# Attention with packed heads: maxima rounded and sums divided on GpSimd, the first causal mask added by the array

## The chip, the cores and the metric

One NeuronCore of a Trainium2 chip runs the whole program in one launch. The metric is the device time in microseconds. Engines are named as the profile names them: PE (TensorE; PEld is its loading of weights), DVE (VectorE), ACT (ScalarE), POOL (GpSimd) and SP (SyncE, which only issues DMAs here).

## The reference

A network of four layers on 2048 tokens of width 128, in float32. Each layer is half a feed-forward block, an attention and half a feed-forward block, each behind a layer norm and added to x. Only the first three attentions are touched:

```python
# attn0: 8 heads of 16, causal, geometry term in the keys; attn1, attn2: 16 heads of 8
scores = q @ k.T * scale            # attn2 with rotary tables
scores = scores + causal            # attn0 only
out = softmax(scores) @ v
x = x + out @ w_out                 # attn1 also + bias
```

The sequence is all 2048 tokens as one in each of them. attn3 (16 heads of 64, causal, with a latent key and value) runs in the same function but isn't changed.

## The kernel before, in words

`packed` prepares attn0, attn1 and attn2 and `flash` runs them. Tokens are taken in 4 chunks of 512. Heads are handled in groups of 4, so an iteration is one group of 4 heads and one chunk of queries: 8 iterations in attn0 (2 groups, heads of 16), 16 in each of attn1 and attn2 (4 groups, heads of 8). Scores are made twice.

The first pass (`stream_a`, `some`) finds the maximum of every row. PE multiplies 128 queries by 512 keys for two heads at once into a pair of PSUM banks, of which there are two pairs (L1071). VectorE reduces a pair to one maximum per row and head (L1089). In attn0's diagonal chunk the last 128 columns must be masked: there VectorE runs, for each head, one operation that adds a strip of zeros and of the mask and takes the maximum (L1081). At the end of an iteration `maxima` reduces the four partial maxima (L1100) and `put_max` writes the negated maximum as a bf16 value and a bf16 remainder into `top` (L1556, L1557). Some program time later `put` lets PE form the shifted queries in a bank named pm, as the queries plus the transposed maxima (L1566, L1570), and ScalarE copies them to q2 (L1574).

The second pass (`stream_b`) makes the scores again with keys on the partitions and the maximum already subtracted (L1213), ScalarE takes the exponential (L1222), and PE multiplies by the values into one accumulator bank (L1159). The products with the values of a key tile are issued in two halves, one key tile later. A column of ones among the values gives the sum of each row. Banks for L1213, for pm and for the transposes are taken in turn out of the same three.

At the end of an iteration `finish` copies the accumulator (L1582, ScalarE). `normal` transposes it into a bank po (L1587), takes the reciprocal of the sums (L1592, VectorE) and multiplies (L1593, VectorE) into `os`, the output with all heads of a chunk. After the last group `out_a` transposes that on PE (L1607) and `out_b` projects it and adds it to x (L1615, L1620).

PE's instructions stay in program order. `flash` writes that order by hand: it keeps a clock of the columns issued so far, takes a step of the first pass whenever that pass is less than an iteration and a bit ahead of the second, and calls pending work (`after(delay, fn)`) once the clock has passed its time. The other engines' order comes from the scheduler, which also follows the few order-only dependencies (`in_order`); every engine then works through its own queue in order. `half_masks` (L1026) is attn3's way to mask: two heads with 64 rows each get the bf16 mask added in their banks by products with an identity, in halves of the rows.

Most lines of the changed file stand 2 to 10 lines away from those of the one before; line numbers here are those of the kernel before.

Of the kernel before, what the change touches and what calls it, by code (L numbers as in the profile page):

```python
# [9 lines left out]
F32 = mybir.dt.float32  # L10
# [54 lines left out]
def tile_macaron(ctx: ExitStack, tc: tile.TileContext, a: dict, out: bass.AP, stages=STAGES):  # L65
# [31 lines left out]
    nc.gpsimd.memset(ones, 1.0)  # L97
    minus_half = const.tile([P, TC], F32, name="minus_half")
    nc.gpsimd.memset(minus_half, -0.5)

    def cs(name):
        return cst[:, slice(*CONSTS[name])]
# [871 lines left out]
    def flash(io, pool, early, its, nh, causal, scale, s1, s2, pv_mm, put_max, begin, finish, poll=None,  # L974
# [7 lines left out]

        halved = nh == 2
        clock = [0.0]
        total = [0]
        later = []

# [7 lines left out]
        def after(delay, fn):  # L995
            later.append((clock[0] + delay, fn))
            later.sort(key=lambda v: v[0])
# [7 lines left out]
        def chunks(qc):  # L1005
            return qc + 1 if causal else NC

        if halved:

            halves = {}  # L1010
            for name in ("ident", "maskq", "maskk"):
                raw = pool().tile([P, 2, P], F32, name="halfraw", tag="halfraw", bufs=2)
                for j in range(2):
                    nc.sync.dma_start(
                        out=raw[P // 2 * j : P // 2 * (j + 1)],
                        in_=a["consts"][:, slice(*CONSTS[name])].rearrange("(b i) k -> i b k", b=2),
                    )
                halves[name] = pool().tile([P, 2, P], BF16, name="half" + name)
                nc.vector.tensor_copy(halves[name], raw)

        def half_masks(outs, mask):

            for b in range(2):
                for j in range(2):
# [1 line left out]
                    pe(nc.tensor.matmul(  # L1026
                        outs[j], halves["ident"][s, b], halves[mask][s, b], start=False, stop=b == 1
                    ))

        if tiled and causal:  # L1030
            junk = pool().tile([P, CH], F32, name="junk")
            strip = pool().tile([P, CH], F32, name="strip")
            nc.gpsimd.memset(strip[:, : CH - P], 0.0)
            nc.vector.tensor_copy(strip[:, CH - P :], cs("maskq"))

        ready = set()
        alive = [True]
# [16 lines left out]
        def some(n, turns, mp):  # L1054

            g, qc = its[n]
            nk = chunks(qc)
            for first, (r, kcs) in enumerate(turns):
                before = hook(n, kcs[0], r) if hook is not None else None
                if first == 0 and before is None:  # L1060
                    before = newest[0]
                for kc in kcs:
                    for j0 in range(0, nh, 2):
                        ps = first_pass_bank()
                        last = causal and kc == qc
                        masked = last and not tiled
                        w = (r + 1) * P if last else CH
                        for j in range(2):
                            o = j * CH
                            lhsT, rhs = s1(n, j0 + j, r, kc)  # L1070
                            pe(nc.tensor.matmul(  # L1071
                                ps[:, o : o + w], lhsT, rhs[:, :w], start=True, stop=not masked
                            ))
                            pos[0] += w
                        if masked:
                            half_masks([ps[:, j * CH + w - P : j * CH + w] for j in range(2)], "maskq")
                        both = ps.rearrange("p (j n) -> p j n", j=2)
                        with tc.high_priority() if not waiting[0] else nullcontext():
                            if last and tiled:
                                for j in range(2):  # L1080
                                    ins = nc.vector.tensor_tensor_reduce(  # L1081
                                        junk[:, :w], both[:, j, :w], strip[:, CH - w :], 1.0, NEG,
                                        ALU.add, ALU.max, mp[:, r, j0 + j, kc : kc + 1],
                                    )
                                    if before is not None:
                                        in_order(ins, before)
                                        before = None
                            else:
                                ins = nc.vector.tensor_reduce(  # L1089
                                    mp[:, r, j0 : j0 + 2, kc], both[:, :, :w], AX.X, ALU.max,  # L1090
                                )
                        if before is not None:
                            in_order(ins, before)
                            before = None
                        yield 2 * w if tiled else w

        def maxima(n, mp):
            nk = chunks(its[n][1])
            mx = pool().tile([P, TC, nh], F32, name="mx", tag="mxa", bufs=3)
            nc.vector.tensor_reduce(mx, mp[:, :, :, :nk], AX.X, ALU.max, negate=True)  # L1100
            put, newest[0] = put_max(n, mx, pe)

            def done():
                put()
                ready.add(n)

            after(2000.0, done)

        newest = [None]
        waiting = [False]  # L1110
# [214 lines left out]
    def packed(io, early, hd, causal, scale, project, w, wv, wo, bias=None, outs=True):  # L1325
# [222 lines left out]
            o = (kt * 4 + j) * slot  # L1548
            return vt[its[n][0]][:, o : o + 32], slice(32 * j, 32 * j + 32)

        def put_max(n, mx, pe):
            top = tops[n % 3]
            tv = top.rearrange("p a r (j s) -> p a r j s", s=span)[:, :, :, :, 3:8:4]
            for i in range(nq):
                m = mx[:, :, i * per : (i + 1) * per]
                nc.vector.tensor_copy(tv[:, i, :, :, 0], m)  # L1556
                last = nc.vector.tensor_tensor(  # L1557
                    tv[:, i, :, :, 1], m, tv[:, i, :, :, 0], ALU.subtract
                )

            def put():

                t = room[0].tile([P, nq, CH], F32R, name="q2", tag="q2", bufs=3)
                for i in range(nq):
                    ps = bank("pm")
                    pe(nc.tensor.matmul(  # L1566
                        ps, masks_b["ident_r"], qt[its[n]][:, i, :], start=True, stop=False
                    ))
                    for r in range(TC):
                        pe(nc.tensor.matmul(  # L1570
                            ps[:, r * P : (r + 1) * P], top[:, i, r, :], masks_b["ident_b"],
                            start=False, stop=r == TC - 1,
                        ))
                    nc.scalar.copy(t[:, i, :], ps)  # L1574
                q2[its[n]] = t

            return put, last

        def finish(n, pv, after, pe):
            g, qc = its[n]  # L1580
            ov = room[1].tile([P, CH], F32, name="ov", tag="ov", bufs=2)
            nc.scalar.copy(ov, pv)  # L1582

            def normal():
                ps = bank("po")
                for r in range(TC):
                    pe(nc.tensor.transpose(  # L1587
                        ps[:, r * P : (r + 1) * P], ov[:, r * P : (r + 1) * P], ident
                    ))
                po = ps.rearrange("p (r j m) -> p r j m", r=TC, j=4)  # L1590
                rc = room[0].tile([P, TC, 4], F32, name="rc", tag="rc", bufs=2)
                nc.vector.reciprocal(rc, po[:, :, :, hd])  # L1592
                nc.vector.tensor_tensor(  # L1593
                    os[qc][:, :, g * 4 * hd : (g + 1) * 4 * hd].rearrange(
                        "p r (j d) -> p r j d", j=4
                    ),
                    po[:, :, :, :hd],
                    rc.unsqueeze(3).to_broadcast([P, TC, 4, hd]),
                    ALU.mult,
                )  # L1600
                if g == n_groups - 1:
                    after(OUT_A if causal else 1500.0, out_a)

            def out_a():
                ps = bank("oT")
                for i in range(TC):
                    pe(nc.tensor.transpose(ps[:, i * P : (i + 1) * P], os[qc][:, i, :], ident))  # L1607
                oT = room[1].tile([P, CH], F32, name="oT", tag="ov", bufs=2)
                nc.scalar.copy(oT, ps)
                after(1500.0, lambda: out_b(oT))  # L1610

            def out_b(oT):
                ps = bank("py").rearrange("p (i c) -> p i c", i=TC)
                for i in range(TC):
                    pe(nc.tensor.matmul(  # L1615
                        ps[:, i, :], oT[:, i * P : (i + 1) * P], wo, start=True, stop=True
                    ))
                if bias is not None:
                    nc.gpsimd.tensor_tensor(xs[qc], xs[qc], over(bias, TC), ALU.add)
                nc.vector.tensor_tensor(xs[qc], xs[qc], ps, ALU.add)  # L1620
                io.mark(qc)

            after(1500.0, normal)
# [766 lines left out]
```

## Time and profile before

| | |
|---|---|
| time of three runs, median (lowest to highest) | 3719.4 us (3716.38 to 3719.66) |
| the profiled execution's own time | 3720.81 us |
| its span, first to last instruction | 3719.1 us |
| mean granted PE clock | 0.950 |
| attn0, about 178 to 455 us | 277 us |
| attn1, about 793 to 1484 us | 691 us |
| attn2, about 1679 to 2391 us | 712 us |
| a maximum over two heads of 512 (L1089) | 1344 of them, 1219 ns each |
| masked maxima of attn0 (L1081) | 128 of them, 0.29 to 0.69 us each |
| exponential of 512 (L1222) | 2272 of them, 609 ns each |
| rounding of maxima in attn1 and attn2 (L1556, L1557) | 32 of each, about 0.20 and 0.23 us |
| reciprocal and product in attn1 and attn2 (L1592, L1593) | 32 of each, 0.26 and 0.29 us |

In the profile's groups the columns are line, engine, operation, output and inputs with their shapes, the count, the busy time in us with the mean of one in ns, and the idle time of the engine just ahead of such instructions, with what ended it. In a timeline they are start, length, engine, line, operation; a bracket gives idle time and what ended it. Neighbours of one line are merged ("x7"), and two instructions of one engine may overlap by some tens of ns, so that the spacing of starts, not the length of one, tells the pace.

### The profile page before, as it was taken

How to read it: one execution, taken by the hardware profiler on the slowest of the kernel's cores; microseconds unless marked ns; L12 is line 12 of the kernel's file. 1: busy time of each engine (PE TensorE's matmuls, PEld its weight loads, DVE VectorE, ACT ScalarE, POOL GpSimd, SP SyncE). 2: the span in 40 equal slices, each digit the busy share in tenths (PEclk: the TensorE clock that was granted, in tenths of full speed). 3: DMA queues.
4: the chain of work that ended last, by engine and by line, in shares of the span. 5: the costliest groups of instructions: out<-in, count | busy, mean ns of one | idle time of the engine just before them, and what ended most of it. 6: DMA issues, size and time to landing. Idle time of an engine off the chain costs nothing. (4 is left out here: it accounts for less than half of the span.)

```text
span 3719.1 us, 64518 instructions
## 1 busy us (share of the span) xinstructions
PE 3404.5 (92%) x25325; PEld 1837.3 (49%) x25325; DVE 2853.9 (77%) x4729; ACT 2025.6 (54%) x3815; POOL 817.1 (22%) x816
## 2 busy tenths in 40 slices
PE   7689987989999999997999999898889999999989
PEld 5543366854333333883333333376444444445457
DVE  6588556778999995778999999544777877788852
ACT  3346722317888888333888888731333344444442
POOL 1511124000000000210000000232555445533341
PEclk9779989979999999996999999898999999999999
DMA  3420123000000000100000000012443232211010
GB/s 106 98 52 14 37 62 91 7 20 9 15 6 16 6 4 7 55 25 21 10 16 10 12 6 1 26 44 68 151 146 112 96 106 98 97 57 52 24 35 12
DMA packets 124977, 170.18 MB, mean 46 GB/s; under 512 B 25152, under 2 KB 52930, under 8 KB 124672
## 3 DMA queue, kind: packets, MB, share of 16 engines
q1 hardware_dynamic: 122112, 160.80, 13.8%
q0 software_dynamic: 2560, 5.25, 0.9%
q8 instruction: 199, 3.26, 0.4%
q14 instruction: 106, 0.87, 0.1%
HBM read 101.25 MB, written 45.87 MB: 40 GB/s over the span
## 5 line engine op out<-in xcount | busy, mean ns | idle before, releaser
L1089 DVE TENSOR_REDUCE mp<-s 128x2 f32<-128x1024 f32 (+3 forms) x1440 | 1627.7, 1183 | 80.2 <-PE s L1071 56.7
L1222 ACT ACTIVATE pt<-s 128x512 f32<-128x512 f32 (+1 forms) x2368 | 1220.5, 601 | 217.7 <-PE s L1213 165.2
L1213 PE MATMUL s<-q,km 32*128 32x512 f32 (+2 forms) x2368 | 735.0, 493 | 28.8 <-ACT pt L1222 18.6
L1159 PE MATMUL pv<-pt,v 128*32 128x256 f32 (+1 forms) x8568 | 732.2, 414 | 22.9 <-ACT ov L1582 11.2
L1071 PE MATMUL s<-km,qt 32*128 32x512 f32 (+3 forms) x2368 | 617.1, 506 | 64.9 <-DVE mp L1089 45.3
L1213 PEld LDWEIGHTS s<-q,km 32*128 32x128 f32 (+1 forms) x2368 | 323.9, 184 | 531.4 <-issue 339.5
L1202 ACT ACTIVATE pt<-s 128x512 f32<-128x512 f32 (+3 forms) x640 | 306.3, 530 | 361.3 <-PE s L1194 216.3
L143 POOL TENSOR_TENSOR rs<-rs,minus_half 128x4 f32<-128x4 f32 x56 | 57.3, 1023 | 1491.8 <-DVE rs L142 1468.1
L2071 DVE TENSOR_TENSOR sum<-sum,pt 128x512 f32<-128x512 f32 (+3 forms) x328 | 260.0, 808 | 86.9 <-ACT pt L1202 85.6
L1159 PEld LDWEIGHTS pv<-pt,v 128*32 128x32 f32 x8568 | 169.2, 108 | 317.7 <-issue 147.1
L1194 PE MATMUL s<-q,k 64*128 64x512 f32 (+3 forms) x1920 | 295.1, 400 | 14.9 <-ACT pt L1202 10.5
L1159 PE MATMUL pv<-pt,latv 128*64 128x512 f32 (+3 forms) x1280 | 307.5, 560 | 1.3 <-ACT pt L1202 1.3
L2071 POOL TENSOR_TENSOR sum<-sum,pt 128x512 f32<-128x512 f32 (+1 forms) x200 | 264.7, 1324 | 179.8 <-ACT pt L1202 176.4
L1071 PEld LDWEIGHTS s<-km,qt 32*128 32x128 f32 (+1 forms) x2368 | 236.2, 191 | 123.8 <-DVE mp L1089 82.3
L1194 PEld LDWEIGHTS s<-q,k 64*128 64x128 f32 x1920 | 159.1, 186 | 222.8 <-issue 140.5
L715 ACT ACTIVATE sg<-pg 128x1024 f32<-128x1024 f32 x72 | 74.0, 1027 | 158.2 <-PE pg L229 142.0
L1071 PE MATMUL s<-k,q 64*128 64x512 f32 (+3 forms) x640 | 131.9, 430 | 19.0 <-DVE mp L1089 18.8
L1873 DVE TENSOR_TENSOR rot<-rot,tab 128x512 f32<-128x512 f32 x128 | 87.8, 686 | 74.8 <-PE rot L229 43.3
L725 PEld LDWEIGHTS pd<-l1d,h 128*128 128x128 f32 x1152 | 139.0, 191 | 5.6
L725 PE MATMUL pd<-l1d,h 128*128 128x128 f32 x1152 | 139.8, 275 | 0.0
L717 DVE TENSOR_TENSOR h<-pu,sg 128x1024 f32<-128x1024 f32 x72 | 87.8, 1220 | 51.7 <-PE pu L229 46.5
L1888 ACT CAST h<-rot 128x512 fp32r<-128x512 f32 x64 | 39.6, 619 | 159.5 <-POOL rot L1883 159.5
(572 smaller groups left out, 4736.3 us busy)
## 6 DMA issues: line engine op xcount, KB each, us to landing
tab<-in_l3rope SPq DMA_DIRECT2D x66, 256.0 KB
q<-q SPq DMA_DIRECT2D x32, 512.0 KB
k<-k SPq DMA_DIRECT2D x32, 512.0 KB
l0e<-in_l0e SPq DMA_DIRECT2D x32, 256.0 KB
q<-h SPq DMA_DIRECT2D x32, 256.0 KB
q<-rot SPq DMA_DIRECT2D x32, 256.0 KB
k<-h SPq DMA_DIRECT2D x32, 256.0 KB
k<-rot SPq DMA_DIRECT2D x32, 256.0 KB
```

Source lines behind the costliest of these rows:

```text
L715: nc.scalar.activation(sg, pg, AF.Silu)
L717: nc.vector.tensor_tensor(h.rearrange("p m n -> p (m n)"), pu, sg, ALU.mult)
L725: nc.tensor.matmul(pd[:, i, :], h[:, m, i * P : (i + 1) * P], wd[:, m, :], start=m == 0, stop=m == 1,)
L1071: pe(nc.tensor.matmul(ps[:, o : o + w], lhsT, rhs[:, :w], start=True, stop=not masked))
L1089: ins = nc.vector.tensor_reduce(mp[:, r, j0 : j0 + 2, kc], both[:, :, :w], AX.X, ALU.max,)
L1159: i = pe(nc.tensor.matmul(pv[out_rows, lo:hi], lhsT, pts[j][:, lo:hi], start=kt == 0, stop=kt == nt - 1 and hi == CH))
L1194: pe(nc.tensor.matmul(outs[j][:, c0:], lhsT, rhs[:, c0:], start=i == 0, stop=i == len(terms[0]) - 1 and not diag,))
L1202: ex = nc.scalar.activation(pts[j][:, c0:], outs[j][:, c0:], AF.Exp, scale=scale)
L1213: pe(nc.tensor.matmul(ps[:, c0:], lhsT, rhs[:, c0:], start=i == 0, stop=i == len(terms) - 1 and (tiled or not diag),))
L1222: ex = nc.scalar.activation(pt[:, c0:], ps[:, c0:], AF.Exp, scale=scale)
L1873: nc.vector.tensor_tensor(t.bitcast(F32), ps, halves["tabs"][i], ALU.mult)
L2071: eng.tensor_tensor(t[:, c0:], other[:, c0:], pts[j][:, c0:], ALU.add)
```

## The change

In attn0 the diagonal banks of the first pass are masked by `half_masks`, as in attn3, and reduced like all others, two heads at once. The junk and strip tiles go; two masks in bf16 are loaded and cast when attn0 begins.

In attn1 and attn2, from the second iteration on, `put_max` runs on GpSimd, and the put of the shifted queries is due 3000 instead of 2000 ns of program time after the maxima. In all iterations but the last, `normal` lets ScalarE copy the transposed accumulator out of PSUM, and GpSimd raises the sums to the power of -1 and multiplies.

```diff
+    minus_one = const.tile([P, TC, 4], F32, name="minus_one")
+    nc.gpsimd.memset(minus_one, -1.0)
...
+        aside = tiled and not causal
...
-        if halved:
+        if causal:
             halves = {}
-            for name in ("ident", "maskq", "maskk"):
+            for name in ("ident", "maskq", "maskk")[: 3 if halved else 2]:
...
-        if tiled and causal:
-            junk = pool().tile([P, CH], F32, name="junk")
-            strip = pool().tile([P, CH], F32, name="strip")
-            nc.gpsimd.memset(strip[:, : CH - P], 0.0)
-            nc.vector.tensor_copy(strip[:, CH - P :], cs("maskq"))
...
-                        masked = last and not tiled
+                        masked = last
...
-                            if last and tiled:
-                                for j in range(2):
-                                    ins = nc.vector.tensor_tensor_reduce(
-                                        junk[:, :w], both[:, j, :w], strip[:, CH - w :], 1.0, NEG,
-                                        ALU.add, ALU.max, mp[:, r, j0 + j, kc : kc + 1],
-                                    )
...
-                            else:
-                                ins = nc.vector.tensor_reduce(
-                                    mp[:, r, j0 : j0 + 2, kc], both[:, :, :w], AX.X, ALU.max,
-                                )
+                            ins = nc.vector.tensor_reduce(
+                                mp[:, r, j0 : j0 + 2, kc], both[:, :, :w], AX.X, ALU.max,
+                            )
...
-            nc.vector.tensor_reduce(mx, mp[:, :, :, :nk], AX.X, ALU.max, negate=True)
-            put, newest[0] = put_max(n, mx, pe)
+            newest[0] = nc.vector.tensor_reduce(mx, mp[:, :, :, :nk], AX.X, ALU.max, negate=True)
+            if aside and n:
+                put, _ = put_max(n, mx, pe, nc.gpsimd)
+            else:
+                put, newest[0] = put_max(n, mx, pe)
...
-            after(2000.0, done)
+            after(3000.0 if aside and n else 2000.0, done)
...
-        def put_max(n, mx, pe):
+        def put_max(n, mx, pe, eng=nc.vector):
...
-                nc.vector.tensor_copy(tv[:, i, :, :, 0], m)
-                last = nc.vector.tensor_tensor(
-                    tv[:, i, :, :, 1], m, tv[:, i, :, :, 0], ALU.subtract
-                )
+                eng.tensor_copy(tv[:, i, :, :, 0], m)
+                last = eng.tensor_tensor(tv[:, i, :, :, 1], m, tv[:, i, :, :, 0], ALU.subtract)
...
+                if causal or n == len(its) - 1:
...
+                else:
+                    ot = room[1].tile([P, CH], F32, name="ot", tag="ov", bufs=2)
+                    nc.scalar.copy(ot, ps)
+                    po = ot.rearrange("p (r j m) -> p r j m", r=TC, j=4)
+                    rc = room[0].tile([P, TC, 4], F32, name="rc", tag="rc", bufs=2)
+                    nc.gpsimd.tensor_tensor(rc, po[:, :, :, hd], minus_one, ALU.pow)
+                    nc.gpsimd.tensor_tensor(
+                        out, po[:, :, :, :hd],
+                        rc.unsqueeze(3).to_broadcast([P, TC, 4, hd]), ALU.mult,
+                    )
```

More of the change, by code (lines that the diff above doesn't have):

```diff
@@ L1078, in some @@
                         with tc.high_priority() if not waiting[0] else nullcontext():
-                            if last and tiled:
-                                for j in range(2):
-                                    ins = nc.vector.tensor_tensor_reduce(
-                                        junk[:, :w], both[:, j, :w], strip[:, CH - w :], 1.0, NEG,
-                                        ALU.add, ALU.max, mp[:, r, j0 + j, kc : kc + 1],
-                                    )
-                                    if before is not None:
-                                        in_order(ins, before)
-                                        before = None
-                            else:
-                                ins = nc.vector.tensor_reduce(
-                                    mp[:, r, j0 : j0 + 2, kc], both[:, :, :w], AX.X, ALU.max,
-                                )
+                            ins = nc.vector.tensor_reduce(
+                                mp[:, r, j0 : j0 + 2, kc], both[:, :, :w], AX.X, ALU.max,
+                            )
                         if before is not None:
@@ L1589, in normal @@
                     ))
[L1590 to L1599, printed above, removed]
-                )
+                out = os[qc][:, :, g * 4 * hd : (g + 1) * 4 * hd].rearrange(
+                    "p r (j d) -> p r j d", j=4
+                )
+                if causal or n == len(its) - 1:
+                    po = ps.rearrange("p (r j m) -> p r j m", r=TC, j=4)
+                    rc = room[0].tile([P, TC, 4], F32, name="rc", tag="rc", bufs=2)
+                    nc.vector.reciprocal(rc, po[:, :, :, hd])
+                    nc.vector.tensor_tensor(
+                        out, po[:, :, :, :hd], rc.unsqueeze(3).to_broadcast([P, TC, 4, hd]), ALU.mult
+                    )
[3 more added lines that the diff above has]
+                    po = ot.rearrange("p (r j m) -> p r j m", r=TC, j=4)
+                    rc = room[0].tile([P, TC, 4], F32, name="rc", tag="rc", bufs=2)
+                    nc.gpsimd.tensor_tensor(rc, po[:, :, :, hd], minus_one, ALU.pow)
+                    nc.gpsimd.tensor_tensor(
+                        out, po[:, :, :, :hd],
+                        rc.unsqueeze(3).to_broadcast([P, TC, 4, hd]), ALU.mult,
+                    )
                 if g == n_groups - 1:
```

## The prediction

> **What bounds the kernel.** I read the page's engine totals first, then the busy time by stage, then inside one stage the timeline, and last who waited for whom there. On the page TensorE looks full and the row maxima (L1089) are the costliest group:
>
> ```profile
> PE 3404.5 (92%) x25325; PEld 1837.3 (49%) x25325; DVE 2853.9 (77%) x4729; ACT 2025.6 (54%) x3815; POOL 817.1 (22%) x816
> L1089 DVE TENSOR_REDUCE mp<-s 128x2 f32<-128x1024 f32 (+3 forms) x1440 | 1627.7, 1183 | 80.2 <-PE s L1071 56.7
> ```
>
> The change acts in the first three attentions. By stage (columns: length, busy us and instructions of PE, PEld, DVE, ACT, POOL, then clock, DMA), attn0, attn1 and attn2 are:
>
> ```profile
> 178.00:455.00 277.00, 242.18 (x1809) 106.00 (x1810) 201.11 (x484) 171.53 (x359) 40.32 (x132) 0.89 0.11 29
> 793.00:1484.00 691.00, 655.55 (x6096) 259.29 (x6097) 624.66 (x692) 561.57 (x1079) 9.50 (x13) 0.96 0.04 9
> 1679.00:2391.00 712.00, 661.66 (x6127) 260.52 (x6128) 646.82 (x735) 564.75 (x1092) 23.18 (x22) 0.94 0.04 10
> ```
>
> In attn1 and attn2 PE and VectorE are both near 90% busy, so the shares don't tell which of them sets the pace. VectorE alone, over two iterations of attn1:
>
> ```profile
> 1189.36 8.12 DVE L1089 TENSOR_REDUCE mp<-s 128x2 f32<-128x1024 f32 x7
> 1197.51 0.22 DVE L1100 TENSOR_REDUCE mx<-mp 128x16 f32<-128x64 f32 x1
> 1197.77 0.20 DVE L1556 CAST top<-mx 128x16 bf16<-128x16 f32 x1
> 1198.01 0.23 DVE L1557 TENSOR_TENSOR top<-mx,top 128x16 bf16<-128x16 f32 x1
> 1198.11 8.01 DVE L1089 TENSOR_REDUCE mp<-s 128x2 f32<-128x1024 f32 x7
> 1206.84 0.26 DVE L1592 RECIPROCAL rc<-po 128x16 f32<-128x16 f32 x1 [0.72 <-PE po L1587]
> 1207.13 0.29 DVE L1593 TENSOR_TENSOR o<-po,rc 128x128 f32<-128x128 f32 x1
> 1207.34 28.71 DVE L1089 TENSOR_REDUCE mp<-s 128x2 f32<-128x1024 f32 x25
> ```
>
> Seven maxima end to end take 8.01 us just after an interruption, a spacing of (8.01-1.22)/6 = 1.13 us; before it they take 8.12, a spacing of 1.15. So VectorE can go at 1.13 and is held to 1.15 by something else. Who waits, over 400 us of the steady part:
>
> ```profile
> PEld pv L1159 <- ACT pt L1222: 45.2, 144, 0.9
> ACT pt L1222 <- PE s L1213: 30.6, 105, 1.2
> DVE rc L1592 <- PE po L1587: 5.5, 8, 0.7
> PE s L1213 <- DVE o L1593: 2.6, 8, 0.3
> DVE mp L1089 <- PE s L1213: 1.3, 2, 1.1
> ```
>
> PE waits for ScalarE's exponentials and ScalarE for PE; no row of that answer has the score products of L1071 waiting for a maximum. The ring is seen in the timeline:
>
> ```profile
> 1191.08 0.49 PE L1213 MATMUL s<-q,km 32*128 32x512 f32 x1
> 1191.67 2.06 ACT L1222 ACTIVATE pt<-s 128x512 f32<-128x512 f32 x4 [0.23 <-PE s L1213]
> 1192.81 0.16 PEld L1159 LDWEIGHTS pv<-pt,v 128*32 128x32 f32 x8 [0.31 <-ACT pt L1222]
> 1193.37 0.18 PEld L1213 LDWEIGHTS s<-q,km 32*128 32x128 f32 x1 [0.41 <-issue]
> ```
>
> A score product at 1191.08, its exponential at 1191.67, the second exponential 0.49 later, its end 0.59 after that and the value products at 1192.81, the next score product at 1193.37: 2.30 us a key tile. VectorE needs 2 x 1.13 = 2.26. An iteration is 16 tiles, 36.8 us; the copies of the output accumulator (L1582) are 38.5 us apart, so 1.7 us go at its seam. **VectorE has little room, but in the steady iterations it is not last.** It is last in short stretches: L1071 follows the end of a maximum by 0.06 us for part of 880 to 932 and of 1370 to 1438 us (attn1), and of 2268 to 2300 (attn2). In attn0 it is last before 202 us:
>
> ```profile
> PEld s L1071 <- DVE mp L1081: 14.2, 13, 2.9
> PE s L1071 <- DVE mp L1081: 9.9, 13, 2.6
> ```
>
> **Part by part.** The sum is made against the profiled execution (span 3719.1, 3720.8 in all); the shown runs' median is 1.4 lower, and I subtract that at the end.
>
> *attn0, masks on the array.* In 64 diagonal banks two masked maxima (mean 0.69, 0.55, 0.42 and 0.29 us at widths 512 to 128, with an accumulator read of 0.08 each) become one plain maximum over both heads (1.22, 0.94, 0.68, 0.41 by attn3's rows, of which 0.09 overlaps the next). Per set of widths 2 x (1.95 + 4 x 0.04) = 4.2 us against 2.9: with 16 sets VectorE is relieved of 21 us. PE gets 256 bf16 mask products. In attn3 the same four, in two concurrent pairs, hold PE about 0.1 us a bank at full clock: 6 us. Before 202 us VectorE is the bound, with 16 banks; but there PE must refill two banks at a clock of 0.55, so by alternation of the two I get a bank every 0.95 us on average, where 1.18 are seen: 3.6 us gained. The mask constants, now four small DMAs amid SP's loads of y and two casts (0.28 each in attn3) ahead of the layer norm, give back 0.6. From 202 to 415 us about 30% of L1071's banks wait for VectorE: a third of 48 x 0.3 us gained, and the masks' 5 us where PE leads lost: about nothing. Together -3 us; bounds -9 (the masks hidden) and +3 (no relief after 202).
>
> *attn1 and attn2, rounding of the maxima to GpSimd, in 30 iterations.* VectorE loses a cast and a subtraction, 0.34 us between their starts and the next maximum. Nothing waits for that in the ring. GpSimd's copies: its additions give 1373 ns at 512 elements and 1064 at 384, so 2.4 ns an element and 0.14 to start; 16 elements are 0.2 us each, done long before use. But the put is also due 1000 ns later, and the built order shows what that does: the five products that make the shifted queries (pm, 0.66 us) move behind the next four score products. Before, pm ran at 1198.98 while PE would have waited anyway: the ring's next turn came at 2.73 instead of 2.29 us, a cost of 0.43. After, pm takes the bank of a score whose exponential ends at 1199.66, exactly when the value products are free to go: all of 0.66 lands on the ring. +0.23, and the two quicker turns (2.24) that followed the old place become one: +0.05.
>
> *The division, from a ScalarE copy.* VectorE is freed of 0.50 us and of 0.72 us of waiting. Its bank was given back at 1207.43; a ScalarE copy (0.59, as L1582) can start at 1206.87 and end at 1207.46: the same. ScalarE is idle then (1.18 us before 1207.27), but the next exponential is 0.07 late. So a steady seam costs 0.23 + 0.05 + 0.07 = 0.35 us; some 24 of them: **+8.4 us** (0 if pm finds cover, +12). In the stretches where VectorE leads, the freed time comes back: about 2 us early in attn1 and four times 0.34 late: **-3.4** (-7 to -2). ScalarE bounds the last iteration of each stage, and one copy falls in it: +1.
>
> *Who waits for GpSimd.* VectorE's quotient was ready at 1362.45 and the transposes of out_a (L1607) followed at 1363.43, in PE's fixed order. Now: copy to 1362.5, power, product, transposes. L143, the near row, takes 1.02 us for 4 elements a partition; 16 cost 1.0 if all of it is a fixed start, 3.7 if 0.14 is and the rest goes with the elements. I take 2.5, in the middle, for a function that works element by element. The product: the Trainium skill (GPSIMD Engine Reference, Engine selection) puts such work on VectorE, GpSimd being about twice as slow with two inputs; that makes 0.58 of VectorE's 0.29. The row for the same 512-element addition is 1373 against 1121, only 1.2 times; the slope above gives 0.45, and I take that: 0.1 us lies between them. Transposes at 1362.5 + 2.5 + 0.5 + 0.15 = 1365.6, 2.2 us late; PE has 0.3 of waiting there and ScalarE's queue some in the tail, so 1.6. Three iterations of the last group in each of two stages (the fourth keeps the old path): **+9.6 us** (2 to 18). Behind the transposes stand all of PE's products, and through them ScalarE and the maxima. In the other iterations nobody reads the quotient soon.
>
> *A lock.* The skill's page SBUF — State Buffer (SBUF: two separate sides) has VectorE and GpSimd block each other on a shared port when VectorE has two SBUF inputs. By that rule each GpSimd step could hold VectorE, up to 3.5 us an iteration and 105 in all; by the rows VectorE is reading PSUM with one input then, so I enter nothing.
>
> Sum: -3 + 8.4 - 3.4 + 1 + 9.6 = +12.6; 3720.8 + 12.6 - 1.4 = **3732 us**.
>
> **Rivals.** *All covered:* the power costs its 1.0 (stalls 6 x 0.4), pm loses only 0.1, the masks hide (-6): -6 + 2.4 - 3.4 + 2.4 + 1 = -3.6, 3716 us. For it: GpSimd is 1% busy in attn1. Against: the order of pm.
> *VectorE was the bound after all:* the 1.56 us freed in 30 seams are 47 us; if the ring tightens when the maxima don't interrupt and half returns, with -9 in attn0, 3687 us. It decides if maxima that start earlier let score products start earlier. For it: VectorE is 98% busy between seams. Against: no such wait in the 400 us.
> *The power goes with its elements (3.7) and the masks cost PE fully:* 6 x 3.1 and +3: 18.6 + 3 + 8.4 - 3.4 + 1 = +28, 3747 us.
>
> **Chances.** The forecast 0.5, all covered 0.25, VectorE the bound 0.13, the long power 0.12. A measurement can tell about 0.2% (7.4 us) from no change. Faster is the third case and a little of the second, 0.18; within 0.2% most of the second and the lower edge of the first, 0.26; slower 0.56. The range reaches down into the second case and a few us past it, and up to the fourth: 3706 to 3747; the forecast's own is 3722 to 3742.
>
> **What would show it.** L1071 in attn1 waits for maxima no more than before and the spacing of maxima stays 1.15; copies of the accumulator 38.8 to 39.0 us apart; pm directly ahead of value products; L1607 waiting for GpSimd by 0.7 to 3.4 us; the power's own row; maxima of attn0 at 0.3 to 1.1 us, and attn0 shorter by some 3 us. Wrong would be accumulator copies under 38.3 us apart, or a power under 1.2 us.

## The result, and the profile after

The changed kernel takes 3737.7 us (median of six runs, 3735.9 to 3745.0) against 3716.2 for the kernel before (median of six, 3711.8 to 3719.7): a ratio of 1.0062, with a 95% interval of 1.0049 to 1.0075. It is slower by 18 to 28 us; the forecast was 3732, 12.6 us above the 3719.4 from which it was reckoned. The profiled execution took 3737.09 us, with a span of 3735.3 against 3719.1. The forecast is close in part by luck: attn0 gained more than its term and the last groups lost more than theirs, and the two errors partly cancel.

The page of the changed kernel has the same engines full, more on GpSimd, and the new operations with their own rows. The rounding (L1548) costs 0.25 us a piece, the power (L1595) 2.9:

```profile
PE 3419.9 (92%) x25581; PEld 1848.4 (49%) x25581; DVE 2823.0 (76%) x4418; ACT 2036.1 (55%) x3845; POOL 934.8 (25%) x936
L1077 DVE TENSOR_REDUCE mp<-s 128x2 f32<-128x1024 f32 (+1 forms) x1504 | 1683.1, 1168 | 146.4 <-PE s L1069 72.8
L1548 POOL CAST top<-mx 128x16 bf16<-128x16 f32 x30 | 7.6, 254 | 752.0 <-DVE mx L1088 666.0
L1595 POOL TENSOR_TENSOR rc<-ot,minus_one 128x16 f32<-128x16 f32 x30 | 87.1, 2905 | 272.8 <-ACT ot L1592 272.8
```

The three stages, cut at the same places of the program as before (length, busy us of PE, PEld, DVE, ACT and POOL, clock, DMA):

```profile
178.00:445.00 267.00, 242.31 (x2078) 115.31 (x2077) 194.49 (x307) 172.37 (x362) 41.34 (x133) 0.94 0.12 31
782.50:1490.50 708.00, 665.42 (x6097) 259.83 (x6097) 615.08 (x637) 567.43 (x1094) 67.10 (x73) 0.95 0.03 9
1687.50:2416.50 729.00, 672.62 (x6128) 263.72 (x6129) 634.61 (x675) 570.08 (x1104) 79.71 (x80) 0.93 0.04 9
```

attn0 lasts 267 us instead of 277, attn1 708 instead of 691, attn2 729 instead of 712. VectorE has less to do in attn1 and attn2 and both are longer. The copies of the output accumulator (L1572) stand at the same place of every iteration, so they tell where the time goes. The table gives the length of a stretch between two of them before, and its change in the profile of the changed kernel, in us:

| stretch (copies) | before | changed kernel |
|---|---|---|
| attn0, first to last of 8 | 228.4 | -10.5 |
| attn1, third to twelfth of 16 (9 seams) | 347.9 | +3.0 |
| attn1, thirteenth to sixteenth (last group of heads) | 122.7 | +13.3 |
| attn2, first to twelfth (11 seams) | 427.8 | +7.3 |
| attn2, thirteenth to sixteenth (last group of heads) | 131.6 | +9.5 |

The middle row is read from these two copies, 9 iterations and 351.0 us apart, where the kernel before has 347.9:

```profile
961.16 0.59 ACT L1572 COPY ov<-pv 128x512 f32<-128x512 f32 x1
...
1312.13 0.59 ACT L1572 COPY ov<-pv 128x512 f32<-128x512 f32 x1 [1.19 <-PE pv L1151]
```

Where the last groups lose it is plain in the timeline of the first of them, attn1:

```profile
1355.12 0.58 ACT L1592 COPY ot<-po 128x512 f32<-128x512 f32 x1 [0.81 <-PE po L1577]
...
1355.78 2.90 POOL L1595 TENSOR_TENSOR rc<-ot,minus_one 128x16 f32<-128x16 f32 x1 [9.25 <-ACT ot L1592]
...
1358.76 0.40 POOL L1596 TENSOR_TENSOR o<-ot,rc 128x128 f32<-128x128 f32 x1
1359.22 0.64 PEld L1606 LDWEIGHTS oT<-cst,o 128*128 128x128 f32 x4 [2.78 <-POOL o L1596]
1359.22 1.04 PE L1606 MATMUL oT<-cst,o 128*128 128x128 f32 x4 [2.47 <-POOL o L1596]
...
1360.19 1.08 PE L1151 MATMUL pv<-pt,v 128*32 128x256 f32 x8
```

Copy, power, product and transposes follow one another without a gap, and PE stands still for 2.47 us. Then look at the lengths: the four transposes take 1.04 us and eight value products 1.08. In the kernel before the same transposes follow the work ahead of them without a gap and take 0.66, and four of the value products behind them take 0.42 (all eight 0.64):

```profile
1363.43 0.66 PE L1607 MATMUL oT<-cst,o 128*128 128x128 f32 x4
1364.02 0.42 PE L1159 MATMUL pv<-pt,v 128*32 128x256 f32 x4
```

PE comes back at about half speed. Columns as in the stages above:

```profile
1356.60:1359.20 2.60, 0.15 (x1) 0.00 (x0) 1.29 (x2) 1.07 (x3) 2.49 (x2) 1.00 0.00 0
1359.20:1362.60 3.40, 3.38 (x24) 1.33 (x24) 0.54 (x1) 1.16 (x3) 0.00 (x0) 0.52 0.00 0
```

The granted clock is 1.00 during the wait and 0.52 in the 3.4 us behind it; behind the second wait it is 0.51 from 1407 to 1414 us. Such a stretch follows five of the six waits, and 22 of the 24 in the four profiled executions that have the late transposes in full (this one and three further on). Over all six, PE waits 15.1 us for the product on GpSimd. That leaves about 8 of the 22.8 us for the clock and whatever else differs.

### The profile page after: what moved, and what is told of

It is laid out like the page before. It is cut to its first block, busy times and chain, and to the rows that moved or that the text cites. A ratio compares the mean times of both kernels' runs of the same rounds, so it can differ in the third digit from the quotient of the medians.

```text
span 3735.3 us, 64855 instructions
## 1 busy us (share of the span) xinstructions
PE 3419.9 (92%) x25581; PEld 1848.4 (49%) x25581; DVE 2823.0 (76%) x4418; ACT 2036.1 (55%) x3845; POOL 934.8 (25%) x936
## 5 line engine op out<-in xcount | busy, mean ns | idle before, releaser
L1077 DVE TENSOR_REDUCE mp<-s 128x2 f32<-128x1024 f32 (+1 forms) x1504 | 1683.1, 1168 | 146.4 <-PE s L1069 72.8
L1069 PE MATMUL s<-km,qt 32*128 32x512 f32 (+3 forms) x2368 | 614.8, 505 | 53.4 <-DVE mp L1077 50.5
L1069 PEld LDWEIGHTS s<-km,qt 32*128 32x128 f32 (+1 forms) x2368 | 234.8, 190 | 108.2 <-DVE mp L1077 94.2
L1548 POOL CAST top<-mx 128x16 bf16<-128x16 f32 x30 | 7.6, 254 | 752.0 <-DVE mx L1088 666.0
L145 POOL TENSOR_TENSOR rs<-rs,minus_half 128x4 f32<-128x4 f32 x56 | 57.4, 1025 | 432.0 <-DVE rs L144 408.4
L1595 POOL TENSOR_TENSOR rc<-ot,minus_one 128x16 f32<-128x16 f32 x30 | 87.1, 2905 | 272.8 <-ACT ot L1592 272.8
L1069 PE MATMUL s<-k,q 64*128 64x512 f32 (+3 forms) x640 | 130.6, 426 | 17.3 <-DVE mp L1077 17.2
```

Source lines behind the costliest of these rows:

```text
L1069: pe(nc.tensor.matmul(ps[:, o : o + w], lhsT, rhs[:, :w], start=True, stop=not masked))
L1077: ins = nc.vector.tensor_reduce(mp[:, r, j0 : j0 + 2, kc], both[:, :, :w], AX.X, ALU.max,)
L1595: nc.gpsimd.tensor_tensor(rc, po[:, :, :, hd], minus_one, ALU.pow)
```

## The experiments

My theory after reading both profiles: (1) the late transposes make the 22.8 us of the last groups, partly as the wait and partly as half clock behind it; (2) the later put makes most of the seams' cost; (3) VectorE's relief in attn0 makes the gain there. The rivals: the loss lies in ScalarE's extra copy, in GpSimd as such or in the rounding; the time behind a wait is a refilling of the pipeline; attn0's gain is luck, or PE's clock kept up by added products. The sets of runs lie apart in level (the kernel before had medians of 3724.9, 3739.9 and 3738.6 us beside them), so only ratios to it are compared, and stretches within a trace.

### Masks alone

```diff
 # changed kernel, with put_max and the division as in the kernel before
-            if aside and n:
-                put, _ = put_max(n, mx, pe, nc.gpsimd)
...
-            after(3000.0 if aside and n else 2000.0, done)
+            after(2000.0, done)
...
-                if causal or n == len(its) - 1:
+                if True:
```

> The change in the first attention alone (masks added by TensorE, one maximum over two heads), the rest as before. Reading of the trace: copies of the accumulator in the first attention are 10.2 us earlier after the change and stay so, so this alone gives 3716.2 - 10.2 = 3706 us, with the clock of that stage up from 0.89 to about 0.93. Rival, the prediction's size: -3 us, 3713 us, the other 7 us being luck of the clock in one execution.

Ratio 0.9962 (0.9944 to 0.9979). attn0's copies are 8.1 us closer together, the last group of attn1 is unchanged (0.0), and the nine seams are too (-0.2). So attn0 gains, and attn1 loses nothing without the other parts. The stage has a clock of 0.93, where the kernel before has 0.89:

```profile
178.00:447.00 269.00, 244.24 (x2079) 116.39 (x2078) 194.41 (x309) 172.86 (x363) 41.34 (x133) 0.93 0.12 30
```

A second time:

> The run with masks alone once more, beside the others of this set: 12 to 14 us under the kernel before, if the gain in the first attention doesn't depend on the chip. Rival: it was luck of that chip's clock, 0 to 5 us.

Ratio 0.9948 (0.9929 to 0.9967), and again 8.1 us in attn0. It isn't luck of one execution. The times fall by more, 14 and 19 us by these ratios; what goes beyond the 8.1 us lies behind attn0, where this run's instructions are those of the kernel before, and stays unexplained.

### What in attn0 gains

VectorE keeps its masked maxima, PE has the products as well:

```diff
 # masks alone, and in the diagonal banks again
+                            if last and tiled:
+                                for j in range(2):
+                                    ins = nc.vector.tensor_tensor_reduce(
...
```

> The run with masks alone, but VectorE keeps its masked maxima of before, one for each head, so that the mask is added twice (which changes no maximum). It has TensorE's 256 added products without VectorE's relief. Theory that VectorE's relief makes the gain in the first attention: all 8 to 10 us of it go and TensorE's products cost 0 to 6 us more: 3716 to 3722 us. Rival, the added products gain by keeping TensorE's clock up: 3708 us, the clock of that stage still near 0.93.

And the reverse, a plain maximum without any mask in the first pass of attn0:

```diff
-                        masked = last
+                        masked = last and not tiled
```

> The run with masks alone without the mask products: the maxima of the diagonal banks are taken over unmasked scores (which leaves out the first pass's mask, so the subtracted maxima can be larger than they should be). VectorE's relief without TensorE's work. Theory of the prediction's split: 3.6 us to 5 us better than masks alone in that stage, since the 0.1 us of a bank's products is partly on the path. Rival, the products are hidden, or pay for themselves in clock: no change within 1 us in that stage.

Masked twice has a ratio of 1.0001 (0.9980 to 1.0021), and attn0's copies are 5.2 us further apart than before; without masks it is 0.9980 (0.9964 to 0.9996), and 7.4 us closer. The stage of each, in order (the columns as above), first masked twice:

```profile
190.00:472.50 282.50, 251.94 (x2054) 118.47 (x2055) 202.82 (x487) 171.37 (x359) 40.51 (x133) 0.89 0.10 27
```

then without masks:

```profile
186.50:456.00 269.50, 237.08 (x1818) 106.07 (x1818) 193.21 (x302) 171.78 (x362) 41.29 (x133) 0.92 0.11 30
```

Taking the products away gains nothing over having them (7.4 against 8.1 us), so here the rival was right: once VectorE is relieved, the mask products are hidden. (While VectorE keeps its masked maxima, they cost 5.2 us.) VectorE's relief alone is enough for the gain. The rival that the added products keep the clock up falls as a cause: masked twice has the products, and a clock of 0.89 as before. The clock does go with the size. Eleven profiled executions have both parts of the new mask, with the same instructions in attn0: six gained 7.9 to 8.2 us, three 10.5 and two 12.0, at clocks of 0.98, 0.99 and 1.00 from the first accumulator copy to the last (0.94 before). The relief sets both off; how much of the 8.1 us is shorter waits, and how much the higher clock that comes with them, is not parted by these runs.

### The division alone, and the put alone

Both have the new masks. The first has the division of the changed kernel but rounds on VectorE:

```diff
-            if aside and n:
-                put, _ = put_max(n, mx, pe, nc.gpsimd)
...
-            after(3000.0 if aside and n else 2000.0, done)
+            after(2000.0, done)
```

> Masks as in the run above, and the division by GpSimd from ScalarE's copy in all iterations but the last; rounding on VectorE and the put due at 2000 as before. Theory of the late transposes: +22.8 us in the last groups of attn1 and attn2 and 24 x 0.07 for the copy at the seams, together +24.5 over the run with masks alone, so about 3731 us. Rival, the copy costs a seam all of the 0.33 us that the trace shows: +22.8 + 8 = +31, about 3737 us. Rival, the late transposes are not the cause: under 3716 us.

The second rounds on GpSimd, but puts at 2000 and divides on VectorE:

```diff
-            after(3000.0 if aside and n else 2000.0, done)
+            after(2000.0, done)
...
-                if causal or n == len(its) - 1:
+                if True:
```

> Masks of the first attention on TensorE, and the maxima rounded by GpSimd with the put due at 2000; division on VectorE as before. Theory that no stretch of attn1 and attn2 hangs on VectorE: the 0.34 us freed in 30 seams change nothing, within 2 us of the run with masks alone (12 to 14 us under the kernel before). Rival, the prediction's term for stretches where VectorE leads: 3 us under masks alone or better.

The division has a ratio of 1.0045 (1.0030 to 1.0059), some 17 us over the kernel before, with masks that gain 8 us by the trace or 14 by the time of masks alone: the loss is its own. The time alone would not part the two sizes expected; its trace does: the last group of attn1 is 13.2 us longer, as in the changed kernel, and the nine seams only 0.6 longer, so the copy isn't what they pay. The rounding has 0.9949 (0.9931 to 0.9966), beside 0.9948 of masks alone in the same set: no cost or gain of it shows, within some 7 us either way.

### The place of the put

```diff
-            after(3000.0 if aside and n else 2000.0, done)
+            after(2000.0, done)
```

> The changed kernel, but the put of the shifted queries is due at 2000 again, with the rounding still on GpSimd. Theory of the prediction: the later place of the put costs 0.28 us of the 0.35 at each of some 24 seams: -6.7 us, 3731 us, and the accumulator copies go from 38.9 back to 38.6 us apart. Rival, ScalarE's copy of the transposed accumulator is what the seam pays: no change, 3738 us, copies 38.9 apart. Rival, GpSimd's rounding isn't ready at 2000 and TensorE waits for it: slower, 3745 us.

Ratio 1.0028 (1.0012 to 1.0044). The same two copies, of this kernel, are 348.5 us apart:

```profile
961.93 0.59 ACT L1572 COPY ov<-pv 128x512 f32<-128x512 f32 x1
...
1310.45 0.58 ACT L1572 COPY ov<-pv 128x512 f32<-128x512 f32 x1 [1.19 <-PE pv L1151]
```

That is 0.6 us more than before over nine seams, where the changed kernel has 3.0: the place of the put costs (3.0 - 0.6) / 9 = 0.27 us a seam. In its timeline the shifted queries (L1556, L1560) follow value products and come ahead of score products:

```profile
1189.12 0.64 PE L1151 MATMUL pv<-pt,v 128*32 128x256 f32 x8
1189.69 0.51 PE L1556 MATMUL pm<-qt,ident_r 128*128 128x512 f32 x1
1190.04 0.40 PE L1560 MATMUL pm<-ident_b,top 128*128 128x128 bf16 x4
1190.37 0.50 PE L1205 MATMUL s<-q,km 32*128 32x512 f32 x1
```

In the changed kernel they stand directly ahead of value products:

```profile
1190.55 0.49 PE L1205 MATMUL s<-q,km 32*128 32x512 f32 x1
1191.04 0.51 PE L1556 MATMUL pm<-qt,ident_r 128*128 128x512 f32 x1
1191.39 0.40 PE L1560 MATMUL pm<-ident_b,top 128*128 128x128 bf16 x4
1191.72 0.64 PE L1151 MATMUL pv<-pt,v 128*32 128x256 f32 x8
```

The changed kernel itself, beside others of a set:

> The changed kernel itself beside the others of this set: 21 us over the kernel before as in the first comparison (ratio 1.005 to 1.0075), so that the later put costs some 7 to 10 us over the same kernel with the put due at 2000 (ratio 1.0028). Rival, the later put costs nothing and the ratio here is 1.003.

Ratio 1.0046 (1.0030 to 1.0062), nine seams 2.9 us longer. The intervals of this and of the put at 2000 overlap, so the times alone would not settle 7 us; the seams within the traces do.

### The late transposes

First, VectorE divides in the last group only:

```diff
-                if causal or n == len(its) - 1:
+                if causal or g == n_groups - 1:
```

> The changed kernel, but the four iterations of the last group of heads keep the reciprocal and the product on VectorE from PSUM. Theory: the 22.8 us that attn1 and attn2 lose in their last groups are the transposes of the output waiting for GpSimd and TensorE's half clock after each wait; all of it goes: 3737.7 - 22.8 = 3715 us. Rival, only the six waits of 2.5 us go and the half clock has another cause: 3722 us. Rival, the loss in the last group comes from the rounding of the maxima and the later put: no change, 3738 us.

Ratio 0.9980 (0.9965 to 0.9995), 0.8% below the changed kernel's first result, a little more than expected. The last group of attn1 is 1.6 us longer than before instead of 13.3, that of attn2 4.1 shorter instead of 9.5 longer (masks alone: 2.8 and 1.8 shorter there). The rivals that put the loss on the rounding or the put fall.

Three more kernels, all with the put at 2000, keep something on GpSimd. The transposes are moved behind other work of PE:

```diff
-                    after(OUT_A if causal else 1500.0, out_a)
+                    after(OUT_A if causal else 1500.0 if n == len(its) - 1 else 6000.0, out_a)
```

> The changed kernel with the put due at 2000, and with the transposes of the output put 6000 instead of 1500 ns of program time behind the division (some 16 of TensorE's groups later), in the six iterations where they waited. GpSimd still divides. Theory: what the last groups lose is that wait and the half clock behind it, so both go: copies of the accumulator stay where the run with masks alone has them, within 3 us, and the time is that run's, about 3707 (10 to 14 us under the kernel before). Rival, GpSimd's division hurts in another way (its port, the copy on ScalarE): at most a third of the 18 us comes back, over 3725 us.

PE is kept busy through the wait, with work that no result depends on:

```diff
                 ps = bank("oT")
+                if not causal and n != len(its) - 1:
+                    for _ in range(4):
+                        for i in range(TC):
+                            pe(nc.tensor.transpose(ps[:, i * P : (i + 1) * P], ident, ident))
```

> The changed kernel with the put due at 2000, and sixteen transposes of the identity into the same bank ahead of the transposes of the output, in the six iterations where they wait, so that TensorE works through the 2.5 us instead of idling (no part of the result comes from them). Theory that the wait is paid twice: the wait stays, but no half clock follows; per wait 1.5 to 3.5 us less, 9 to 20 us less in all than the same kernel without them, about 3724 us. Rival, the time behind the wait is lost for another reason (the pipeline fills again): the same 3737 us; and longer, if the transposes take more than the wait.

The power is taken out of the last group's chain:

```diff
-                    nc.gpsimd.tensor_tensor(rc, po[:, :, :, hd], minus_one, ALU.pow)
+                    if g == n_groups - 1:
+                        nc.vector.reciprocal(rc, po[:, :, :, hd])
+                    else:
+                        nc.gpsimd.tensor_tensor(rc, po[:, :, :, hd], minus_one, ALU.pow)
```

> The changed kernel with the put due at 2000; in the last group's iterations the reciprocal of the sums is taken by VectorE from ScalarE's copy, and only the product is left on GpSimd. Theory that the power's 2.9 us are the wait: the transposes wait 0 to 0.3 us instead of 2.5, no half clock follows, and the last groups lose under 3 us of their 22: 8 to 12 us under the kernel before, near the run with late transposes. Rival, each hop from ScalarE to GpSimd to TensorE costs by itself: they still wait over 1 us, time no lower than the kernel before.

| kernel | ratio (95% interval) | last group of attn1 | of attn2 |
|---|---|---|---|
| put at 2000, nothing else | 1.0028 (1.0012 to 1.0044) | +13.2 | +9.2 |
| PE kept busy | 0.9997 (0.9978 to 1.0016) | +7.2 | +4.3 |
| transposes later | 0.9968 (0.9951 to 0.9984) | +0.8 | -1.6 |
| reciprocal on VectorE | 0.9951 (0.9933 to 0.9970) | +0.9 | +1.2 |

The last group of attn1, from its first accumulator copy to its last, is one row for each kernel, with the clock third from the right. The kernel before:

```profile
1359.50:1482.20 122.70, 118.78 (x984) 46.72 (x980) 84.48 (x144) 103.16 (x199) 4.04 (x4) 1.00 0.00 1
```

Put at 2000, with the waits:

```profile
1350.80:1486.80 136.00, 125.71 (x984) 49.30 (x981) 81.94 (x134) 104.78 (x203) 14.99 (x14) 0.94 0.00 1
```

PE kept busy through the waits:

```profile
1367.50:1497.50 130.00, 124.95 (x1032) 51.70 (x1029) 82.11 (x134) 104.74 (x203) 15.02 (x14) 1.00 0.00 1
```

Reciprocal on VectorE:

```profile
1364.00:1487.60 123.60, 120.08 (x984) 46.48 (x981) 82.49 (x137) 104.28 (x202) 6.31 (x11) 0.99 0.00 1
```

With PE kept busy, the transposes are as late as ever, but the clock stays at 1.00, and 6.0 of the 13.2 us are gone; the other 7.2 are the three delays, and the 0.8 that the kernel with later transposes has too. Without the added work the group has 17.1 us of half clock: 3.4 behind each of the three waits, and 6.8 behind a gap of 1.15 us that every kernel has there, some with and some without a drop of the clock; so not all of the 6.0 need belong to the waits. In attn2 the same step saves 4.9 us. Its timeline shows the transposes of the output (L1610) at full speed, 0.66 us, where idling left 1.04:

```profile
1371.60 1.97 PE L1608 MATMUL oT<-cst 128*128 128x128 f32 x16
1373.62 0.41 POOL L1596 TENSOR_TENSOR o<-ot,rc 128x128 f32<-128x128 f32 x1
...
1374.08 0.66 PE L1610 MATMUL oT<-cst,o 128*128 128x128 f32 x4 [0.51 <-POOL o L1596]
```

So the refilling rival falls: the waits are paid twice, in attn1 some 2.1 to 2.4 us each by standing and up to 2.0 us each (1.6 in attn2) by the half clock behind. The two other kernels remove both. The one with the reciprocal came out lower than expected, by some 6 us, and so did masks alone in the same set (19 us under the kernel before instead of 12 to 14), so that is rather the set's level than the reciprocal's. Moved behind other work, the whole division on GpSimd costs 0.8 us in that group. With the reciprocal on VectorE the hop through GpSimd remains, and the transposes wait at most 0.8 us. It is the power's length that makes them late, not GpSimd as such.

## Why the prediction was right, and where not

*The ring.* Right. L1069 waits for maxima in attn1, up to the last group, 30.4 us at its weight loads and 15.6 at its products, against 29.8 and 16.0 before; nearly all of it lies ahead of 900 us, and from 900 to 1300 us it is 0.5 us after and nothing before. A maximum over two heads takes 1221 ns there against 1220. The rival in which VectorE was the bound is out: the rounding moved alone shows no gain, and the seams of the changed kernel are longer although VectorE was freed at each.

*The seam, 0.23 + 0.05 + 0.07 = 0.35.* Right in place and size. The put's place costs 0.27 us against 0.28; ScalarE's copy, from the division with the put at 2000, costs (0.6 + 0.2) / 9 = 0.09 against 0.07, measured from masks alone. The accumulator copies are 39.0 us apart on average, as forecast.

*attn0, -3.* The sign was right, the size wrong: -8.1 in most executions, -10.5 in the profiled one, on either side of the bound of -9 that was given for hidden masks. Three terms failed. The banks from 202 us on were given only a third of 48 x 0.3 us of relief, and the mask products were charged 5 us "where PE leads"; the runs show that they cost nothing there once VectorE is relieved. The 3.6 us of the first 16 banks did come: from the first maximum to the reduction of the second group 18.3 us instead of 21.9. First the kernel before, then the changed one:

```profile
180.13 0.29 DVE L1081 CUSTOM_DVE_ANT_0 junk<-s,strip 128x128 f32<-128x128 f32 x1
202.02 0.18 DVE L1100 TENSOR_REDUCE mx<-mp 128x16 f32<-128x16 f32 x1
```

```profile
185.24 0.42 DVE L1077 TENSOR_REDUCE mp<-s 128x2 f32<-128x256 f32 x1
203.51 0.18 DVE L1088 TENSOR_REDUCE mx<-mp 128x16 f32<-128x16 f32 x1
```

But that first maximum is 5.1 us later. From the first split of the keys (kL) to it, 14.0 us pass instead of 9.3, so the start of the stage lost 4.7 us where the forecast gave back 0.6. Every run that loads the mask constants has this delay, also masked twice and without masks; which of the loads, the casts or the new order of VectorE's queue makes it wasn't tried. So the first accumulator copy is at 220.8 us, against 220.4 before, and all of the net gain is between the first copy and the sixth.

*Stretches where VectorE leads, -3.4.* Failed: with the rounding moved alone, the first two seams of attn1 are 0.1 us shorter than with masks alone, and its last group is 1.7 longer. That a score product follows the end of a maximum by 0.06 us showed that it waited, not that the end of the stage hung on it.

*The transposes, 6 x 1.6 = +9.6.* Right in mechanism, too small. The power was put at 2.5 us and takes 2.9; the product 0.45 and takes 0.40. I forecast 2.2 us of delay, and took off a part as covered by waits that PE has anyway. The traces show 2.5 us standing at each, with nothing covered, and the half clock, which the sum didn't hold at all although the trace of the kernel before shows it behind waits of 2.1 us (the last section has the lines): 22.8 us in the two last groups, where the terms that met there (9.6, +1 and some of -3.4) gave about 7 to 10.

*The lock.* Nothing was entered, and the unchanged 1221 ns bear that out for these operations.

So +15.6 on seams, stretches and last groups became about +36 in the profiled execution, 3.7 of it the open piece below, and -3 in attn0 became -10.5. The sum against the trace, -10.5 + 3.0 + 13.3 + 7.3 + 9.5 and 2.8 for the seams and gaps between, is +25.4 at the last copy of attn2. The profiled execution ends only 16.3 us later, because attn3 and what lies around it, which the change doesn't touch, ran 9 us quicker in it. In the twelve other traces that unchanged part lies between 11.1 us shorter and 0.4 us longer than in the profile before, so it varies by as much from execution to execution.

One piece stays open. In attn2 3.7 of the 7.3 us fall at one seam, where PE runs at half clock for 10.2 us from 1919.1 us on (0.56 over the row below, which starts and ends later) although in the 15 us ahead of it no product of PE waited for over 0.6 us:

```profile
1920.60:1930.60 10.00, 9.75 (x72) 3.25 (x68) 6.82 (x6) 6.15 (x12) 1.76 (x2) 0.56 0.00 0
```

Four of the five kernels with the put at 2000 and the power on GpSimd lose 3.4 to 6.9 us at one seam of attn2 in the same way, the twelfth; masks alone, run twice, doesn't. The place isn't fixed either: the second profile of the changed kernel has such a loss at the twelfth seam of attn1 (3.7) and of attn2 (3.6) and none at this one, and the rounding alone has one of 2.3. In each trace the changes of the clock lie on a grid of 3.41 us, and a half-clock stretch lasts 3.4 us or a whole multiple of it. A seam a little emptier for PE may be enough where it falls badly on that grid, but no run isolates that.

No version beats masks alone (0.9962 and 0.9948): with the reciprocal on VectorE in the last group it is 0.9951, with the rounding on GpSimd 0.9949, too close to be told apart.

## What to carry to other kernels

Before work moves to an engine that is idle, look for who reads the result next in program order: here 24 of 30 divisions had an iteration to spare, and the other six made most of the loss. Where a nearly always busy PE must stand for 2 to 3 us, as here, count the half clock behind it too, or give it other work first. And a score product that starts right behind a maximum doesn't show that VectorE sets the pace: in attn1, where the other ring takes 2.30 us a key tile to VectorE's 2.26, freeing VectorE gained nothing that these runs can show.

## What was not expected of the hardware

PE dropped to half clock after standing for 2.47 us, for 3 to 7 us, with a load of about 90% around it. The kernel before shows the same in the last iterations of attn2, where PE waits 2.12 us for an exponential (the wait, then the stretch behind it):

```profile
2358.20:2360.30 2.10, 0.01 (x2) 0.01 (x2) 0.51 (x1) 2.10 (x6) 0.47 (x1) 1.00 0.00 0
2361.30:2368.10 6.80, 6.80 (x36) 2.10 (x32) 3.66 (x7) 4.94 (x10) 1.27 (x1) 0.50 0.01 2
```

The Trainium skill (TensorE: Matmul & The Clock Gate, HAM oscillation) warns of gaps above some 3.4 us; by that rule these waits would have cost nothing more than themselves, and by the run that keeps PE busy they cost up to 2.0 us more each. The measurement decides: shorter gaps can do it.

GpSimd's power takes longer with more elements: 4 elements a partition take 1.025 us (L145) and 16 take 2.905. A straight line through these two sizes has 0.157 us an element and 0.40 to start (an estimate; no third size was run). Its cast and subtraction of 16 elements take 0.25 and 0.27, against 0.20 and 0.23 on VectorE, and its product of 128 elements takes 0.40 against 0.29.
